# Two scratch tiles of their own, two loads traced later, and the last chunk of the output in halves, in a four-layer graph network kernel

## The chip, the cores and the metric

The kernel runs on one core of a Trainium2 chip. The time is that of the device in microseconds. Before the change it is 1733.46 us, the median of 3 runs (1733.0 to 1734.63).

## What is computed

Four layers on x [8, 2048, 64] with one adjacency `adj` [2048, 2048] of zeros and ones; after each layer `x = layernorm(x + layer(x))`. Cut to what matters here:

```python
# layer 0: hypergraph attention over H [2048, 64], and a mean over neighbours
industry = (adj / max(adj.sum(-1), 1)) @ (x @ W_ind)      # inverse degrees
g        = softmax-weighted sum over hyperedges of elu(beta * h + (1 - beta) * agg)
out      = softmax over the pair (industry, g), mixed
# layer 1: D^-1/2 (A + I) D^-1/2 x W^T
# layer 2: x, A x, (2 A A - I) x and softmax(relu(emb emb^T)) x, with weights made from emb per node
# layer 3: three steps of v = relu([v, adj @ v] W1^T + b1) W2^T + b2
```

## The kernel before, in words

**Tiling.** The eight batches are taken as four pairs p = 0..3, so that a pair's features fill 128 partitions. The 2048 nodes are 16 tiles of 128 (t) or 4 chunks of 512 (c). The product of an operand with `adj` runs over the 16 tiles, for two chunks at a time (g = 0, 1, both chunks in the two halves of one PSUM tile `ug` [128, 2, 512]), and twice over, for a rounded part `v{c}h` and its remainder `v{c}l` (`split`, L162).

**Order of the work.** The program traces instructions in the order in which the Python code makes them; a planner then orders each engine's queue, and lets an instruction that it takes to be ready pass others. `tc.keep_in_program_order` (in the code `pin`, and within `mm` and `transpose`) holds an instruction behind the one that was traced before it on the same engine. All matmuls are held that way. The loads by `load_emb` (L1066) and `load_xn` (L1027), and the instructions of `inverses` (L359), are not. `after(n, ...)` and `later(n, ...)` trace a piece n `tick`s later; a tick follows each matmul of a product.

**Stages, in order of time.** (1) Up to about 222 us, layer 0's attention: per tile and slot, TensorE adds three matmuls into `pz`, VectorE, ScalarE and GpSimd finish them (L815 to L825), and between them TensorE does the products of x with adj (`products`, L342) as filler. Within it `inverses` makes 1/sqrt(deg+1) (`dinv`, a power on GpSimd, L367) and 1/max(deg,1) (L368, L369), both through one tile `deg1`; later it turns the latter with TensorE and stores it (`inv_hbm`). (2) Up to about 470 us, the mixing of layer 0's two parts (`mix_*`, the loop at L1085, 16 steps), with the rest of the products and layer 1 (`layer1`, L1034) as filler. SyncE loads what a step needs: `uts`, `invs`, `gn`, `rs`. Ahead of the loop SyncE also loads the first chunk of the embeddings (`et`, L1073), which `make_er` and `make_el` round after the mixing. (3) Layer 1's tail; x after layer 1 goes to memory as `x2_hbm[p]` (L1018), and `load_xn` fetches it back into `xn[p]` over ScalarE's queue. (4) Layer 2: the softmax product, the products with adj (`supports`, L1262) with small pieces beside them (`aside`), among them `make_est` (L1352), which splits the embeddings for the per-node weights. Its tile `e_hi` takes its place in turn with all tiles of the tag `ut` (two buffers), which hold what leaves PSUM on its way to memory (`out_t`, L1231). Then the per-node weights and their products. (5) Layer 3, from about 1275 us: for each pair three steps of products, and in the last step `rectified` (L1840) and `finish` (L1726): a matmul of four blocks into `po`, the sum with x, a layernorm (L134) and two stores.

**The very end.** For the last pair's last two chunks (`very_end`, L1873) the two chunks run one after the other, 32 matmuls of 512 columns each:

```python
for mine in ([[c] for c in own] if very_end else [own]):
    for t in range(NT ...):
        for i in range(2):
            for c in mine:
                mm(u[c], lhsT=x_part[t // JT][i][:, t % JT, :], rhs=adj_c(t, c), ...)
    for k, c in enumerate(mine ...):
        rectified(c, u[c], bias, very_end)
        later(6 if very_end else 14 + 8 * k, lambda c=c, h=h[c], p=p: finish(p, c, h))
```

Of the kernel before, what the change touches and what calls it, by code (L numbers as in the profile page):

```python
# [56 lines left out]
def tile_gnn_fast(  # L57
# [41 lines left out]
    def cols(c, n=C):  # L99
        return slice(c * n, (c + 1) * n)  # L100
# [70 lines left out]
    def mm(*args, **kw):  # L171
        tc.keep_in_program_order(nc.tensor.matmul(*args, **kw))  # L172

    def transpose(dst, src):
        tc.keep_in_program_order(nc.tensor.transpose(dst, src, ident))  # L175
# [166 lines left out]
    def products():  # L342

        deg1 = hy.tile([P, NT], F32, name="deg1")

        def degrees(g):
            du = pph.tile([P, 2, C], F32, tag="ph", name=f"du{g}", bufs=2)
            for t in range(NT):
                for i in range(2):
                    mm(  # L350
                        du[:, i, :], lhsT=ones_r, rhs=adj_c(t, 2 * g + i), start=t == 0, stop=t == NT - 1
                    )
                    yield
            for i in range(2):
                c = 2 * g + i
                r = slice(c * P // NCH, (c + 1) * P // NCH)
                evacuate(deg4[r, :], du[r, i, :])

        def inverses():  # L359

            pdc = places["small"]([P, JT, P], "pdc")
            for j in range(JT):
                transpose(pdc[:, j, :], deg4[:, cols(j, P)])
            pdc = pdc.rearrange("p j (c r) -> p c j r", c=NCH)[:, :, :, 0]
            d1 = deg1.rearrange("p (c j) -> p c j", c=NCH)
            nc.vector.tensor_scalar(d1, pdc, 1.0, None, op0=ALU.add)
            nc.gpsimd.tensor_tensor(dinv, deg1, neg_half[:, :NT], ALU.pow)  # L367
            nc.vector.tensor_scalar(d1, pdc, 1.0, None, op0=ALU.max)  # L368
            nc.vector.reciprocal(deg1, deg1)  # L369
            for _ in range(20):  # L370
                yield
            for c in range(NCH):
                pt = places["small"]([P, C], "pinv")
                for j in range(JT):
                    k = c * JT + j
                    transpose(pt[:, cols(j, P)], deg1[:, k:k + 1].to_broadcast([P, P]))
                row = va.tile([P, C], F32, tag="ut", name="inv", bufs=2)
                nc.scalar.copy(row, pt)
                nc.sync.dma_start(inv_hbm[:, cols(c)], row)
                for _ in range(4):  # L380
                    yield

        for p in range(NP):
            for g in range(2):
                own = (2 * g, 2 * g + 1)
                ug = pph.tile([P, 2, C], F32, tag="ph", name="ug", bufs=2)
                u = {c: ug[:, c % 2, :] for c in own}
                turning = inverses() if p == 0 and g == 1 else iter(())
                for t in range(NT):
                    for i in range(2):  # L390
                        for c in own:
                            mm(
                                u[c], lhsT=part[t // JT][i][:, t % JT, :], rhs=adj_c(t, c),
                                start=t == 0 and i == 0, stop=t == NT - 1 and i == 1,
                            )
                            tick()
                            if t > 1:
                                next(turning, None)
                            yield
                    if p == NP - 1 and g == 1 and t % JT == JT - 1:  # L400
                        first_parts(t // JT, free)
                    if p + 1 < NP and t % JT == JT - 1:
                        c = t // JT
                        if g == 1:
                            parts(p + 1, c)
                        if g == 1 and c < 2 or g == 0 and c >= 2:
                            fetch(p + 1, (c + 2) % NCH)
                if p == NP - 1:

                    for t in range(g * NT // 2, (g + 1) * NT // 2):  # L410
                        onto_diagonal(t, nc.gpsimd, ALU.add)
                for c in own:
                    ut = va.tile([P, C], F32, tag="ut", name="ut", bufs=2)
                    nc.scalar.copy(ut, u[c])
                    nc.sync.dma_start(u0_hbm[p][:, cols(c)], ut)
                if p == 0 and g == 0:
                    yield from degrees(0)
                    yield from degrees(1)
# [434 lines left out]
    def wide(c):  # L853
        return slice(c * JT, (c + 1) * JT)
# [172 lines left out]
    def load_xn():  # L1027

        for p in range(NP - 1):
            if room and done[p] == NCH:  # L1030
                done[p] = 0
                nc.scalar.dma_start(xn[p], x2_hbm[p][:])

    def layer1(p):  # L1034

# [30 lines left out]
    def load_emb(c, et):  # L1066

        nc.sync.dma_start(et, emb_4[:, cols(c)])
        return et

    er_scope = ExitStack()
    erp = er_scope.enter_context(tc.tile_pool(name="er", bufs=1))
    ets = [load_emb(0, erp.tile([P, C], F32, tag="er", name="et", bufs=2))]  # L1073
    remaining = filler
    filler = all_pairs()
    mix_load(0)
# [7 lines left out]
    fill(4)  # L1084
    for i in range(steps + 1):  # L1085
        k = 9 if i > NCH else 8
        if i < steps:
            mix_scores(i)
            fill(k)
        if i > 0:  # L1090
            mix_end(i - 1)
            fill(k)
        if i + 1 < steps:
            mix_load(i + 2)
            mix_ind(i + 1)
            mix_g(i + 1)
            fill(k)
        if i < steps:
            mix_weigh(i)
            fill(k)  # L1100
# [250 lines left out]

    def make_est(c):  # L1352
        e = e_parts.pop(c)
        hi = va.tile([P, C], F32R, tag="ut", name="e_hi", bufs=2)
        pin(nc.scalar.copy(hi, e))
        signed_parts(e, e, hi, odd16)
        pin(nc.vector.tensor_scalar(hi, e, flip, None, op0=ALU.mult))
        pin(nc.sync.dma_start(est_hbm[:, cols(c)], hi.bitcast(F32)))
# [364 lines left out]
        xs = xn[p][:, wide(c), :]  # L1723
        nc.gpsimd.tensor_tensor(xs, xs, b2.to_broadcast([P, JT, P]), ALU.add)  # L1724

    def finish(p, c, h):  # L1726
        po = lps.tile([P, JT, P], F32, tag="mm", name="po", bufs=4)
        for j in range(JT):
            mm(po[:, j, :], lhsT=h[:, cols(j, P)], rhs=bd_o, start=True, stop=True)
        r = staged("r")  # L1730
        nc.vector.tensor_tensor(r, po, xn[p][:, wide(c), :], ALU.add)  # L1731
        layernorm(va, grouped(r), grouped(r), centred=True, small=l2, tag="ut", bufs=2)
        for b in range(2):
            (nc.scalar if b and p == NP - 1 and c == NCH - 1 else nc.sync).dma_start(
                out[2 * p + b, c * C:(c + 1) * C, :].rearrange("(t p) f -> p t f", p=P),
                r[:, :, b * F:(b + 1) * F],
            )

# [51 lines left out]
    def opening():  # L1790
# [46 lines left out]
                factor(int(n > 22), h[int(n > 22)], bd_e2, be)  # L1837
        return uo

    def rectified(c, src, bias, at_end):  # L1840
        h[c] = new_h(c)
        if c % 2 == 0 or at_end:
            nc.scalar.activation(h[c], src, AF.Relu, bias=bias)  # L1843
        else:
            nc.vector.tensor_scalar(h[c], src, bias, 0.0, op0=ALU.add, op1=ALU.max)

    waiting = list(waiting)
    for p in range(NP):
# [3 lines left out]
        for step in range(STEPS):  # L1852
# [4 lines left out]
            for g in range(2):  # L1857
                own = (2 * g, 2 * g + 1)
                if p == 0 and step == 0:
                    u = {c: opened[c] for c in own}  # L1860
                else:
                    ug = pph.tile([P, 2, C], F32, tag="ph", name="u", bufs=2)
                    u = {c: ug[:, c % 2, :] for c in own}
                    for c in own:
                        mm(u[c], lhsT=w_v, rhs=h[c], start=True, stop=False)
                        tick()
# [4 lines left out]
                        later(2 if g else 40, prepare)  # L1871

                very_end = last and g == 1 and p == NP - 1  # L1873
                for mine in ([[c] for c in own] if very_end else [own]):
                    for t in range(NT if p or step else 0):
                        if checks and t in (2, 7, 12):
                            check()
# [9 lines left out]
                    for k, c in enumerate(mine if p or step or g else []):  # L1887
                        rectified(c, u[c], bias, very_end)
                        if last:
                            at = 6 if very_end else 14 + 8 * k  # L1890
                            later(at, lambda c=c, h=h[c], p=p: finish(p, c, h))
                        else:

                            at = 8 + 6 * k if g == 1 else 18 + 16 * k
                            later(at, lambda c=c: factor(c, h[c], bd_e2, be))
                if g == 1 and last and p + 1 < NP:
                    factor(NCH - 1, h_next[NCH - 1], bd_e, None)
        h = h_next
# [749 lines left out]
```

## Time and profile before

| | before |
|---|---|
| median of 3 runs | 1733.46 us |
| the profiled execution | 1736.35 us, its span 1734.6 us |
| TensorE matmul busy | 1656.1 us, 95% of the span |
| VectorE, ScalarE, GpSimd busy | 48%, 34%, 33% |
| granted TensorE clock, mean | 0.987 |
| 0 to 60 us | TensorE busy 39.3 of 60 us |
| 60 to 240 us | TensorE 156.8, VectorE 141.8, GpSimd 135.9 of 180 us |
| 240 to 1700 us | TensorE 1440.1 of 1460 us |
| 1700 us to the end | TensorE 19.9 of 34.6 us |

A view of waits has, for each engine and line, who it waited for, with the microseconds in total, the number of times and the longest. A timeline row has start, duration, engine, line, operation, `out<-in` with the shapes, and in brackets the idle time of that engine before it and what ended it. A row of windows has the busy time of PE, PEld (weight loads), DVE (VectorE), ACT (ScalarE) and POOL (GpSimd) in a stretch, then the granted TensorE clock (1.00 is full), the share of DMA and GB/s. L172 is the helper of all matmuls, L175 that of all transposes, so that they are told apart by the names of their tiles.

### The profile page before, as it was taken

How to read it: one execution, taken by the hardware profiler on the slowest of the kernel's cores; microseconds unless marked ns; L12 is line 12 of the kernel's file. 1: busy time of each engine (PE TensorE's matmuls, PEld its weight loads, DVE VectorE, ACT ScalarE, POOL GpSimd, SP SyncE). 2: the span in 40 equal slices, each digit the busy share in tenths (PEclk: the TensorE clock that was granted, in tenths of full speed). 3: DMA queues.
4: the chain of work that ended last, by engine and by line, in shares of the span. 5: the costliest groups of instructions: out<-in, count | busy, mean ns of one | idle time of the engine just before them, and what ended most of it. 6: DMA issues, size and time to landing. Idle time of an engine off the chain costs nothing. (4 is left out here: it accounts for less than half of the span.)

```text
span 1734.6 us, 27974 instructions
## 1 busy us (share of the span) xinstructions
PE 1656.1 (95%) x11196; PEld 1206.1 (70%) x11196; DVE 833.3 (48%) x1532; ACT 589.4 (34%) x1031; POOL 570.6 (33%) x515
## 2 busy tenths in 40 slices
PE   6889899999989999999999999999989999999996
PEld 4667666666664444468788878888767877878775
DVE  7788945677742221210137147777533433433332
ACT  1346523434321212112213267878511222212221
POOL 4678835556534443422023001313210200202001
PEclk9899999999999999999999999999999999999998
DMA  9834334444340000027344467675571111211111
GB/s 351 277 121 127 124 116 138 154 140 145 106 129 6 31 27 4 24 70 291 118 134 131 114 149 158 137 165 129 149 263 48 50 55 43 61 49 43 55 43 39
DMA packets 171180, 195.83 MB, mean 113 GB/s; under 512 B 71536, under 2 KB 116336, under 8 KB 169760
## 3 DMA queue, kind: packets, MB, share of 16 engines
q1 hardware_dynamic: 160096, 154.54, 30.7%
q0 software_dynamic: 8544, 30.68, 5.3%
q10 hardware_dynamic: 2400, 8.72, 1.4%
q8 instruction: 90, 1.47, 0.4%
q14 instruction: 50, 0.41, 0.1%
HBM read 126.72 MB, written 67.17 MB: 112 GB/s over the span
## 5 line engine op out<-in xcount | busy, mean ns | idle before, releaser
L172 PE MATMUL ua<-pt,xn 128*128 128x512 f32 x512 | 230.2, 592 | 1.4 <-DVE pt L1174 1.4
L172 PEld LDWEIGHTS ua<-pt,xn 128*128 128x128 f32 x512 | 96.9, 190 | 111.1 <-issue 104.0
L1539 DVE COPY w_half<-pw 128x512 f32<-128x512 f32 x160 | 109.8, 705 | 87.5 <-PE pw L172 86.7
L1535 ACT COPY w_half<-pw 128x1024 f32<-128x1024 f32 x128 | 129.9, 1015 | 58.4 <-PE pw L172 58.3
L172 PE MATMUL py<-w_half,xg 128*32 128x128 f32 x4096 | 143.0, 280 | 1.7 <-issue 1.7
L172 PE MATMUL u<-adj,v0h 128*128 128x512 f32 x384 | 134.5, 428 | 1.1 <-ACT h L1843 1.1
L172 PE MATMUL u<-adj_more,v2h 128*128 128x512 f32 x384 | 125.3, 404 | 0.0
L172 PEld LDWEIGHTS py<-w_half,xg 128*32 128x32 f32 x4096 | 111.6, 138 | 19.5 <-issue 2.6
L172 PE MATMUL u<-adj,v0l 128*128 128x512 f32 x384 | 125.0, 403 | 0.0
L172 PE MATMUL u<-adj_more,v2l 128*128 128x512 f32 x384 | 123.4, 398 | 0.0
L1180 POOL TENSOR_TENSOR acc<-acc,pt 128x512 f32<-128x512 f32 x60 | 76.5, 1276 | 104.2 <-DVE pt L1174 103.5
L172 PE MATMUL pw<-est,wst 64*128 64x256 f32 x1024 | 110.4, 318 | 0.4 <-ACT w_half L1535 0.4
L1174 DVE TENSOR_SCALAR pt<-pt 128x512 f32<-128x512 f32 x64 | 29.9, 468 | 152.3 <-ACT pt L1173 152.1
L172 PEld LDWEIGHTS pw<-est,wst 64*128 64x128 f32 x1024 | 82.7, 186 | 25.4 <-ACT w_half L1535 18.9
L1752 ACT CAST ar<-fcav 128x512 fp32r<-128x512 f32 x64 | 39.5, 618 | 170.3 <-DMA fcav<-in_adj_t 169.3
L1753 DVE SCALAR_TENSOR_TENSOR ar<-fcav,ar 128x512 f32<-128x512 f32 x64 | 45.5, 710 | 103.4 <-ACT ar L1752 103.4
L1173 ACT ACTIVATE pt<-s 128x512 f32<-128x512 f32 x64 | 38.0, 598 | 164.5 <-PE s L172 164.5
L172 PE MATMUL u<-adj,v1h 128*128 128x512 f32 x288 | 93.7, 403 | 0.0
L172 PE MATMUL u<-adj_more,v3l 128*128 128x512 f32 x288 | 93.1, 398 | 0.2 <-DVE v3l L168 0.2
L172 PE MATMUL u<-adj_more,v3h 128*128 128x512 f32 x288 | 92.7, 400 | 0.0
L172 PE MATMUL u<-adj,v1l 128*128 128x512 f32 x288 | 92.0, 397 | 0.0
L1724 POOL TENSOR_TENSOR x<-x,rows 128x512 f32<-128x512 f32 x16 | 22.6, 1435 | 209.7 <-PE pt L175 127.7
(408 smaller groups left out, 3270.1 us busy)
## 6 DMA issues: line engine op xcount, KB each, us to landing
fcav<-in_adj_t SPq DMA_DIRECT2D x64, 256.0 KB, 3.0
u_hbm<-ut SPq DMA_DIRECT2D x48, 256.0 KB, 2.9
xg<-u_hbm SPq DMA_DIRECT2D x24, 512.0 KB, 7.0
adj<-in_adj_t POOLq DMA_DIRECT2D x16, 512.0 KB, 7.7
adj_more<-in_adj_t POOLq DMA_DIRECT2D x16, 512.0 KB, 7.0
adj_hbm<-adj_more SPq DMA_DIRECT2D x16, 512.0 KB, 6.5
x_hbm<-r SPq DMA_DIRECT2D x28, 256.0 KB, 2.4
hs_hbm<-st ACTq DMA_DIRECT2D x8, 584.0 KB, 6.7
```

Of the source, the lines that this page charges most:

```text
L172: tc.keep_in_program_order(nc.tensor.matmul(*args, **kw))
L1173: nc.scalar.activation(pt, s, AF.Exp)
L1174: nc.vector.tensor_scalar(pt, pt, 1.0, None, op0=ALU.max)
L1180: nc.gpsimd.tensor_tensor(accs[c], accs[c], pt, ALU.add)
L1535: pin(nc.scalar.copy(dst, pw.rearrange("p j o n -> p n (j o)")))
L1539: pin(copy(dst[:, :, 2 * j:2 * j + 2], bank.rearrange("p o n -> p n o")))
L1724: nc.gpsimd.tensor_tensor(xs, xs, b2.to_broadcast([P, JT, P]), ALU.add)
L1752: nc.scalar.copy(ar, seen_a)
L1753: nc.vector.scalar_tensor_tensor(ar.bitcast(F32), seen_a, 1.0, ar.bitcast(F32), op0=ALU.mult, op1=ALU.not_equal, accum_out=left[:, t, k:k ...
```

## The change

- `inverses` gets a second small tile `deg_inv` for 1/max(deg,1); before, it overwrote `deg1`, which the power on GpSimd reads.
- `load_xn` hands its load to `after(14, ...)`, so that it is traced 14 ticks later.
- The load of the first chunk of embeddings is traced within the mixing loop, at step 4, and not ahead of it.
- `e_hi` in `make_est` gets a tile of the pool `l2`, one per chunk (tag `g{c}`), and leaves the turn of `ut`.
- The very last chunk runs in two halves of 256 columns (`last_half`), from a PSUM tile `us` of its own, each half with its own 32 matmuls, its own rectification and its own `finish` over two blocks; `finish` takes a range of blocks. The chunk before it runs alone as before.

In the few words that come with it, the change also names a sooner return of the adjacency. `return_adj` (L1678) and its calls have no line in the diff.

```diff
     def products():
         deg1 = hy.tile([P, NT], F32, name="deg1")
+        deg_inv = hy.tile([P, NT], F32, name="deg_inv")
...
-            d1 = deg1.rearrange("p (c j) -> p c j", c=NCH)
+            d1, di = (d.rearrange("p (c j) -> p c j", c=NCH) for d in (deg1, deg_inv))
             nc.vector.tensor_scalar(d1, pdc, 1.0, None, op0=ALU.add)
             nc.gpsimd.tensor_tensor(dinv, deg1, neg_half[:, :NT], ALU.pow)
-            nc.vector.tensor_scalar(d1, pdc, 1.0, None, op0=ALU.max)
-            nc.vector.reciprocal(deg1, deg1)
+            nc.vector.tensor_scalar(di, pdc, 1.0, None, op0=ALU.max)
+            nc.vector.reciprocal(deg_inv, deg_inv)
...
-                    transpose(pt[:, cols(j, P)], deg1[:, k:k + 1].to_broadcast([P, P]))
+                    transpose(pt[:, cols(j, P)], deg_inv[:, k:k + 1].to_broadcast([P, P]))
...
             if room and done[p] == NCH:
                 done[p] = 0
-                nc.scalar.dma_start(xn[p], x2_hbm[p][:])
+                after(14, lambda p=p: nc.scalar.dma_start(xn[p], x2_hbm[p][:]))
...
-    ets = [load_emb(0, erp.tile([P, C], F32, tag="er", name="et", bufs=2))]
+    ets = []
...
     for i in range(steps + 1):
         k = 9 if i > NCH else 8
+        if i == NCH:
+            ets.append(load_emb(0, erp.tile([P, C], F32, tag="er", name="et", bufs=2)))
...
         e = e_parts.pop(c)
-        hi = va.tile([P, C], F32R, tag="ut", name="e_hi", bufs=2)
+        hi = l2.tile([P, 4, P], F32R, tag=f"g{c}", name="e_hi").rearrange("p a b -> p (a b)")
         pin(nc.scalar.copy(hi, e))
...
-    def finish(p, c, h):
-        po = lps.tile([P, JT, P], F32, tag="mm", name="po", bufs=4)
-        for j in range(JT):
-            mm(po[:, j, :], lhsT=h[:, cols(j, P)], rhs=bd_o, start=True, stop=True)
-        r = staged("r")
-        nc.vector.tensor_tensor(r, po, xn[p][:, wide(c), :], ALU.add)
-        layernorm(va, grouped(r), grouped(r), centred=True, small=l2, tag="ut", bufs=2)
+    def finish(p, c, h, blocks=(0, JT)):
+        first, end = blocks
+        n = end - first
+        po = lps.tile([P, JT, P], F32, tag="mm", name="po", bufs=4)[:, 0:n, :]
+        for j in range(n):
+            mm(po[:, j, :], lhsT=h[:, cols(first + j, P)], rhs=bd_o, start=True, stop=True)
+        r = staged("r")[:, 0:n, :]
+        nc.vector.tensor_tensor(r, po, xn[p][:, c * JT + first:c * JT + end, :], ALU.add)
+        layernorm(va, grouped(r), grouped(r), groups=2 * n, centred=True, small=l2, tag="ut", bufs=2)
         for b in range(2):
-            (nc.scalar if b and p == NP - 1 and c == NCH - 1 else nc.sync).dma_start(
+            (nc.scalar if b and first else nc.sync).dma_start(
...
+    def last_half(k, src):
+        part = slice(k * C // 2, (k + 1) * C // 2)
+        for t in range(NT):
+            for i in range(2):
+                mm(
+                    src, lhsT=x_part[t // JT][i][:, t % JT, :], rhs=adj_c(t, NCH - 1)[:, part],
+                    start=False, stop=t == NT - 1 and i == 1,
+                )
+                tick()
+        dst = h[NCH - 1]
+        nc.scalar.activation(dst[:, part], src, AF.Relu, bias=b1s)
+        later(6, lambda: finish(NP - 1, NCH - 1, dst, (k * JT // 2, (k + 1) * JT // 2)))
...
+                    if last and g == 1 and p == NP - 1:
+                        own = own[:1]
...
-                for mine in ([[c] for c in own] if very_end else [own]):
+                for mine in [own]:
...
+                if very_end:
+                    us = pph.tile([P, 2, C], F32, tag="ph", name="u", bufs=2)[:, :, 0:C // 2]
+                    for k in range(2):
+                        mm(us[:, k], lhsT=w_v, rhs=h[NCH - 1][:, cols(k, C // 2)], start=True, stop=False)
+                        tick()
+                    h[NCH - 1] = new_h(NCH - 1)
+                    for k in range(2):
+                        last_half(k, us[:, k])
```

## The prediction

> **What bounds the kernel now.** I read the page's first part, then all waits of TensorE, then the timeline and the windows round each wait that an edit touches, and last the chain at the end. TensorE is busy 95% of the span, so an edit pays only where TensorE stands. The waits that the edits bear on:
>
> ```profile
> PE pg L175 <- DMA gn<-gs_hbm: 4.0, 1, 4.0
> PE po L172 <- ACT ut L1057: 4.9, 2, 3.7
> PE pn L175 <- ACT ut L1235: 2.0, 1, 2.0
> PE u L172 <- ACT h L1843: 1.1, 1, 1.1
> ```
>
> Behind them stand these rows of the timeline (VectorE at 126, ScalarE at 490 and 836), and then the windows (the seventh number is the granted clock):
>
> ```profile
> 125.93 0.17 DVE L368 TENSOR_SCALAR deg<-pdc 128x16 f32<-128x16 f32 x1 [4.72 <-POOL dinv L367]
> 490.43 1.07 ACT L1057 COPY ut<-u 128x512 f32<-128x512 f32 x2 [7.92 <-issue]
> 835.75 0.59 ACT L1235 COPY ut<-u 128x512 f32<-128x512 f32 x1 [4.38 <-DMA est_hbm<-e_hi]
> ```
> ```profile
> 120.00:125.00 5.00, 3.39 (x16) 2.44 (x15) 1.21 (x2) 1.71 (x3) 4.92 (x4) 1.00 0.01 2
> 125.00:130.00 5.00, 2.81 (x10) 2.14 (x11) 4.07 (x11) 1.85 (x7) 4.05 (x4) 0.88 0.00 0
> 130.00:135.00 5.00, 5.00 (x21) 3.96 (x20) 4.38 (x9) 3.90 (x11) 3.89 (x4) 0.78 0.42 110
> ```
>
> And the chain that ended last, its final part:
>
> ```profile
> 1719.87 0.70 ACT h L1843
> 1720.57 0.04 issue
> 1720.62 1.17 PE po L172 x8
> 1721.79 0.02 issue
> 1721.81 0.70 DVE r L1731
> ...
> 1722.60 0.64 ACT ln_c L149
> 1723.23 0.02 issue
> 1723.26 0.70 DVE ln_v L151
> 1723.96 0.02 issue
> 1723.98 0.18 DVE ln_e L153
> ...
> 1724.79 1.15 POOL ln_r L155
> 1725.94 0.02 issue
> 1725.97 0.69 DVE r L156
> ```
>
> From the last product (ends 1719.84) to 1726.66, 6.82 us, there is no TensorE work but the small `po`; then come the stores and the end, 7.9 us, which nothing here changes much.
>
> **A: `deg_inv`.** One more tile, no instruction more. VectorE's L368 no longer waits for GpSimd's power (2.95 us, 122.95 to 125.90), which stood behind two sums `acc`. VectorE gets back up to 4.72 us; queued behind L368 were `y`, `pz` and the next slots, for which TensorE waited. TensorE's loss there: idle 1.59 and 0.99 us before rows at 126.21 and 127.47, and from the clock in the windows (0.12 + 0.22) x 5 = 1.7 us, together 4.3. But GpSimd is the next one late: it is busy 4.92 of 5 us in 120 to 125 with the same power, and its next `acc` (126.85) can come only 0.95 us sooner; three buffers of `y` let VectorE run ahead of it for a while. Bounds -4.7 and 0; I take the middle of 0.95 and 4.3, rounded up a little: **-2.8**.
>
> **B: `load_xn` 14 ticks later.** The third load waits on ScalarE's queue from 481.6 to 489.98 for the store of x2, and behind it stand the two copies `ut` at 490.43 for which TensorE waits 3.66 us (487.41 to 491.07). The clock then falls to 0.64 and 0.51 till 494: eight `po` and two `u` take 1.72 us, where the like row at 466 takes 0.92, and the next pair 1.00 for 0.56, 1.24 us together. At stake: 4.9. But the load is not held in traced order: the first of the three stands at 473.51, before the matmuls `pb` of 474.80, though it is traced after those of 480.48; and `fcav` for layer 3's checks (L1747) is issued at 458.12. A load goes where the planner finds it ready, and its place in the trace decides only between ready ones. The copies are already traced before it, and it passed them. So I take **0**, with -4.9 as the other end.
>
> **C: `et` inside mixing.** On SyncE, issues run without a gap from 230.07: `bp`, two `bd_w`, `et` at 231.75, `gn` at 232.44. Without `et` ahead, `gn` is issued 0.69 us sooner, and 256 KB less go before it. TensorE stands 4.03 us for it (233.6 to 237.63) and would stand 3.3. `et` then comes after the loads that are traced before it, in SyncE's gap at 235.8 or later; its cast `er` on ScalarE, for which ScalarE waited 5.95 us to 236.46 at no cost, moves with it. In mixing ScalarE has gaps of 2.5 us at each `t`, so at most some 3 us of such a wait come through. The Trainium skill (TensorE: Matmul & The Clock Gate, What's actually happening) has the clock halve after an idle window of about 3.4 us. Here it fell after 4.03 us (0.63, 0.50 and 0.90 in the three windows from 237.6 to 243.0: 0.5 + 1.0 + 0.2 = 1.7 us lost) and after 3.66 us, and stayed 1.00 after the 1.96 us at 836. By the rule a stop of 3.3 us might just escape: -2.4 in all; by the nearest row it doesn't. I take **-0.7**; ends -2.4 and +2.3 (3 us less 0.7).
>
> **D: `e_hi` out of the turn of `ut`.** The copy of 835.75 waited for the store of `e_hi` (issued at 831.34, taking 1.99 us on SyncE). In the new turn its buffer is that of the copy at 826.62, whose store was issued at 827.23, and a store lands in 2.4 us or so; it can go at about 831.4, right behind the one at 830.78. TensorE's 1.96 us go. Next late: the second copy (837.98), which needs the buffer stored at 833.90; it ends at 838.57, and TensorE, 1.96 us earlier than its 840.62, asks at 838.66. It just fits. **-2.0**, ends -2.0 and -1.
>
> **E: the last chunk in halves**, step by step against the rows:
> - Between the last two chunks, starts of matmuls are 1.52 us apart (1709.38, 1710.90) where 0.233 is usual: chunk 3 waits for ScalarE to read chunk 2 out of the same tile. The new `us` is another tile. But `finish` of chunk 2 now follows two own terms and four short matmuls, 1.0 us, and waits 0.3 for `h`. -1.29 + 0.3 = -1.0.
> - 32 matmuls of 512 columns at 0.233 (7.46 us) become 64 of 256. No row has this form. 512 columns take 0.233; 128 columns (`po`, eight in 0.89) 0.111. The skill's figure (same page, Back-to-back issue gap) is N/2.4 + 2.5 ns, 0.109 for 256 and 0.216 for 512, and would make it 7.0 us; but its rule for loads (LDWEIGHTS: 128 columns in 107 ns) speaks against halving, since each load has only half as long to hide. The rows lie above the first figure by 20 ns at 512 columns; 0.107 + 0.02 gives an estimate of 0.13. 64 x 0.13 = 8.3: +0.85; ends -0.5 (0.109) and +2.8 (0.16, the load's 0.053 of streaming unhidden). Own terms: +0.05.
> - The second half must wait for ScalarE to read the first, both being parts of one tile; that a tile's parts are not told apart is seen in `DVE h L1845 <- ACT h L1843` (43.4 us, 10 times: two readers of two chunks, one after the other). A drain of 0.29, 0.03, a relu of 0.38, 0.05, less 0.13: +0.62; 0 if they are told apart.
> - `po` of the first half, four instructions: +0.44.
> - The tail on half the width, from rows with 256 columns (ScalarE `bias<-pb` 0.37, VectorE L1153 0.42): relu -0.32, `po` -0.44, sum -0.28, square -0.26, reduction -0.28, scale -0.27. The power took 1.64 us on 8 columns and 2.95 on 16, so 0.98 on 4: -0.67. Together -2.5. The first half's chain ends 5 us after its product, before the second needs VectorE.
>
> Sum **-1.5**; ends -3.5 and +1.
>
> No line of `return_adj` is changed, so a sooner return is worth nothing. **The sum:** -2.8 + 0 - 0.7 - 2.0 - 1.5 = -7.0. On the profiled execution, 1736.35 (span 1734.6 and 1.75 round it), that is 1729.3; the median of the runs is 2.9 lower, and 1733.46 - 7.0 = **1726.5**.
>
> **The rivals.**
> 1. *The later load does pass behind the copies* (B counts). For it: ScalarE's queue is otherwise free there; against it, the moved loads above. -7.0 - 4.9: **1721.6**.
> 2. *GpSimd takes VectorE's place in A*, and the halves gain nothing. For it: POOL 4.92 of 5 us. -0.95 - 0.7 - 2.0 = -3.6: **1729.9**.
> 3. *The edits don't do what they say*: `et` again ahead of `gn` or its cast in front of a `t`, A and E as in 2. About -1.5: **1732**.
> 4. *Slower: the weight loads of the 64 short matmuls are not hidden at all.* Place: the last 10 us. LDWEIGHTS rows show 0.19 us; 0.19 + 0.107 = 0.30 each costs 64 x 0.17 = 10.9 more than my 0.13. It outweighs all else from 0.13 + 7.0/64 = 0.24 us each. Against it: `po` gets through a load and 128 columns in 0.111. **1737.4**.
>
> **How the numbers follow.** A measurement here tells about 0.2%, 3.5 us, from no change. The likeliest case, 42%: 1726.5, own range 1723.5 to 1729.5. Rival 1: 28%. Rival 2: 20%, half of it within 0.2%. Rival 3: 5%, within. Rival 4: 5%, slower. Faster: 0.42 x 0.95 + 0.28 + 0.10 = 0.78; same 0.17; slower 0.05. The range leaves out rival 4, the lowest third of rival 1 and a little of 2 and 3: 1718 to 1732.
>
> **What would show it.** A: L368 right behind L366, and POOL's idle time round 120 to 135 shrinking. B: whether copies L1057 stand before or behind the third load; a gap of 3.66 us left in TensorE says that nothing moved. C: `gn` issued next to `bd_w`, TensorE's wait near 3.3. D: no wait of `pn` near 836. E: starts of the short matmuls 0.13 us apart, no stop between chunks 2 and 3, one of some 0.6 between the halves, about 4.3 us from the last product to the last sum. I am wrong if new waits of TensorE on ScalarE or VectorE turn up in 240 to 480, from queues ordered anew.

## The result, and the profile after

The changed kernel takes 1727.86 us (median of 16 runs, 1724.46 to 1733.03) where the kernel before, on the same chip, took 1733.36 (16 runs). The ratio is 0.9968, with a 95% interval from 0.9959 to 0.9977: 5.5 us less, between 4.0 and 7.1. That is 1.4 us above the forecast of 1726.5 and inside its range. The profiled execution has a span of 1729.0 us (before 1734.6), and TensorE is busy 1655.4 us of it (1656.1 before): what went are stops of TensorE, not work. The total came out nearly as forecast, but two of its five terms did not, in opposite directions.

**Waits of TensorE after.** As before: what waits, for what, us in total, times, longest.

```profile
PE po L172 <- ACT ut L1058: 5.5, 3, 3.7
...
PE pinv L175 <- DVE y L820: 3.4, 2, 3.1
...
PE u L172 <- DVE v3l L168: 2.0, 1, 2.0
...
PE pg L175 <- POOL v0l L168: 1.1, 1, 1.1
...
PE u L172 <- ACT h L1856: 0.6, 1, 0.6
```

Of the four lines shown of before, `pg` fell from 4.0 us to 1.1 (C), `pn` is gone (D), and `u <- ACT h` is halved, as it now stands between two halves (E). The view puts the 1.1 us down to GpSimd, but `gn` landed at 234.60, 0.14 us before TensorE's start, and in c_et, where the view names `gn`, it was 0.13: `gn` would have held TensorE as long. `po` still waits 3.7 us (B); its third stop, 0.65 us at 357.91, is not there before. Two lines take a new place: `pinv` waits for VectorE (A), and `u` waits for `v3l` at the opening of layer 3.

**Timeline of VectorE and GpSimd after, round edit A.**

```profile
120.61 0.17 DVE L369 TENSOR_SCALAR deg_inv<-pdc 128x16 f32<-128x16 f32 x1
...
132.85 0.68 DVE L816 TENSOR_TENSOR pz<-pz,R 128x512 f32<-128x512 f32 x1
133.45 4.82 DVE L825 TENSOR_TENSOR y<-y,co 128x512 f32<-128x512 f32 x1
...
124.07 3.39 POOL L368 TENSOR_TENSOR dinv<-deg,neg_half 128x16 f32<-128x16 f32 x1
...
133.95 1.31 POOL L168 TENSOR_TENSOR hrl<-hrow,hrh 128x512 fp32r<-128x512 f32 x1
135.19 1.31 POOL L826 TENSOR_TENSOR acc<-acc,y 128x512 f32<-128x512 f32 x1
136.44 1.27 POOL L168 TENSOR_TENSOR v1l<-xc,v1h 128x512 fp32r<-128x512 f32 x1
```

L369 no longer waits: it runs at 120.61, where its like ran at 125.93. But 13 us later one product `y<-y,co`, whose two inputs lie in SBUF, is on record for 4.82 us. The 41 rows of its line have a median of 0.69. In that time GpSimd runs three operations without a gap (133.95 to 137.71), and the row ends 0.56 us behind the last of them. The longest row of the line in the kernel before, 3.45 us, ends 0.56 us behind two such operations too (169.98 and 169.42).

**Windows after, the stretch of edit A** (the last three numbers are granted clock, DMA share and GB/s):

```profile
120.00:125.00 5.00, 4.97 (x26) 3.86 (x25) 4.88 (x13) 2.34 (x6) 4.92 (x4) 1.00 0.01 2
125.00:130.00 5.00, 3.62 (x17) 2.48 (x16) 3.25 (x8) 3.04 (x10) 5.00 (x4) 1.00 0.00 0
130.00:135.00 5.00, 4.54 (x24) 3.51 (x24) 5.00 (x6) 3.10 (x6) 4.39 (x4) 1.00 0.55 168
135.00:140.00 5.00, 1.94 (x12) 1.41 (x11) 5.00 (x5) 1.03 (x2) 3.98 (x4) 0.97 0.41 116
140.00:145.00 5.00, 5.00 (x18) 3.77 (x17) 3.73 (x9) 3.62 (x12) 3.38 (x3) 0.69 0.83 284
```

In 120 to 130 TensorE is busy 8.59 us, before 6.20, and its clock stays at 1.00, before 0.88. In 135 to 140 it is busy only 1.94 us, before 4.91, and then the clock is 0.69. What the first windows win, the last ones give back.

**Timeline of ScalarE after, at edits B and D.**

```profile
486.17 0.33 ACTq L1033 DMA_DIRECT2D xn<-x_hbm  x1
486.61 1.07 ACT L1058 COPY ut<-u 128x512 f32<-128x512 f32 x2 [7.96 <-issue]
...
827.97 0.59 ACT L1238 COPY ut<-u 128x512 f32<-128x512 f32 x1
833.55 0.59 ACT L1238 COPY ut<-u 128x512 f32<-128x512 f32 x1 [4.99 <-DMA xt_hbm<-ut]
```

The third load still stands in front of the two copies (B did nothing). The copy that stood at 835.75 now runs at 827.97, without a wait. The one after it (837.98 before) is that of 833.55; it waits for another store, and TensorE has no wait for it.

**The end of the chain that ended last, after:**

```profile
1710.51 0.48 ACT h L1856
1710.99 0.04 issue
1711.04 0.98 PE u L172 x6
1712.01 0.45 PE po L172 x4
1712.46 3.12 PE u L172 x26
...
1715.60 0.48 ACT h L1856
...
1716.13 0.73 PE po L172 x4
...
1716.88 0.43 DVE r L1736
...
1719.10 0.53 POOL ln_r L155
...
1719.66 0.42 DVE r L156
```

From the last product (1715.58) to the last `r` (1720.08) it is 4.5 us, before 6.8. From there to the end of the span it is 8.9, before 7.9.

**A table by stage.** TensorE runs nearly the same matmuls in all these kernels. So each matmul of one trace can be paired with its like in the trace of before, and the difference of the two starts is the lead that the kernel has there. The table gives by how much the lead changes over each stage (negative is faster; stages by the time of before; each end is the median of the five starts before it; the last stage runs to the end of the span). The third column is the kernel that has that edit alone. The last gives the kernels with one edit that is not this stage's: it shows what one trace differs from another with no cause here.

| stage, us | changed kernel | that edit alone | others |
|---|---|---|---|
| A, 121 to 226 | -0.75 | -0.36 | -0.3 to +1.1 |
| C, 226 to 300 | -3.48 | -3.26 | -0.5 to +0.8 |
| B, 470 to 520 | +0.27 | +1.56 | -0.8 to -0.3 |
| D, 830 to 850 | -2.18 | -2.18 | -0.3 to +1.4 |
| opening of layer 3, 1273 to 1400 | +1.01 | | 0.0 to +1.7 |
| E, 1690 to the end | -1.19 | -1.36 | 0.0 to +0.2 |

The five edits make -7.3 us in the changed kernel. The rest of its -5.5 in the profile: +0.75 already there ahead of 121, the +1.0 of the opening, and next to nothing elsewhere. C, D and E stand clear of the last column. A lies barely under it, the opening lies inside it, and for B the column is too narrow a measure (b_load and c_slot, below).

### The profile page after: what moved, and what is told of

Read it like the earlier page. It is cut to its first block, busy times and chain, and to the rows that moved or that the text cites. A ratio compares the mean times of both kernels' runs of the same rounds, so it can differ in the third digit from the quotient of the medians.

```text
span 1729.0 us, 28043 instructions
## 1 busy us (share of the span) xinstructions
PE 1655.4 (96%) x11230; PEld 1208.0 (70%) x11230; DVE 843.0 (49%) x1536; ACT 589.1 (34%) x1033; POOL 569.9 (33%) x516
## 5 line engine op out<-in xcount | busy, mean ns | idle before, releaser
L172 PE MATMUL u<-adj,v0h 128*128 128x512 f32 (+1 forms) x388 | 135.7, 427 | 0.6 <-ACT h L1856 0.6
L172 PE MATMUL u<-adj,v0l 128*128 128x512 f32 (+1 forms) x388 | 125.8, 402 | 0.0
L172 PE MATMUL u<-adj_more,v2h 128*128 128x512 f32 (+1 forms) x388 | 125.7, 402 | 0.0
L172 PE MATMUL u<-adj_more,v2l 128*128 128x512 f32 (+1 forms) x388 | 124.0, 396 | 0.0
L172 PE MATMUL u<-adj_more,v3l 128*128 128x512 f32 (+1 forms) x291 | 93.5, 396 | 2.1 <-DVE v3l L168 2.0
L172 PE MATMUL u<-adj,v1h 128*128 128x512 f32 (+1 forms) x291 | 94.0, 401 | 0.0
L172 PE MATMUL u<-adj_more,v3h 128*128 128x512 f32 (+1 forms) x291 | 93.1, 398 | 0.0
L172 PE MATMUL u<-adj,v1l 128*128 128x512 f32 (+1 forms) x291 | 92.6, 395 | 0.0
```

## The experiments

All times come with runs of the kernel before on the same chip. The ratio turns them into us of 1733.4. "Theory" in the expectations is the reading of the result before the run:

| kernel | median us (before) | ratio, 95% interval | us |
|---|---|---|---|
| a_deg | 1734.44 (1735.2) | 0.9992 (0.9977 to 1.0006) | -1.4 |
| b_load | 1738.08 (1735.36) | 1.001 (0.9998 to 1.0022) | +1.7 |
| c_et | 1733.18 (1735.2) | 0.9982 (0.9971 to 0.9993) | -3.1 |
| d_ehi | 1733.27 (1735.2) | 0.9983 (0.9966 to 0.9999) | -2.9 |
| e_half | 1733.88 (1735.2) | 0.999 (0.9978 to 1.0002) | -1.7 |
| c_queue | 1731.37 (1735.36) | 0.9981 (0.997 to 0.9992) | -3.3 |
| c_slot | 1731.47 (1736.07) | 0.9979 (0.9969 to 0.9989) | -3.6 |
| f_power | 1727.55 (1735.36) | 0.9953 (0.9938 to 0.9968) | -8.1 |
| g_hold | 1728.32 (1735.36) | 0.9956 (0.9944 to 0.9968) | -7.6 |
| g2_last | 1727.49 (1736.07) | 0.9942 (0.992 to 0.9964) | -10.1 |
| h_consts | 1728.06 (1736.07) | 0.9957 (0.9943 to 0.9972) | -7.5 |
| i_all2 | 1721.92 (1736.07) | 0.9921 (0.9901 to 0.9941) | -13.7 |

An interval is 2 to 4 us wide on either side, which is as much as one edit is worth. So the times decide on the large ones, and the stages of the traces on the others. The five single edits add up to -7.4 us, with B the odd one out.

### Each edit alone: a_deg, b_load, c_et, d_ehi, e_half

Each is the kernel before with one part of the diff above and nothing else.

> Edit A alone, on the kernel before. Theory: TensorE gets ahead by up to 5 us at 132, and loses it again to two- or three-microsecond stops up to 141, because VectorE's sum of two tiles in SBUF is held while GpSimd works through its backlog; net 0 (-1 to +1 us) at the first `pi` near 226, and about 1733 in all. The prediction's term: -2.8, that is about 1730.5. Should the gain be lost in the whole change only because something else of it got in between, this run keeps -2.8 or more.

Its lead at 121, 132, 141 and 226 is -3.54, -8.69, -2.69 and -3.90: it wins 5.2 us, loses 6.0, and finds 1.2 again on the way to `pi`, the first products of mixing, near 226: -0.36 in all. The same course stands in the changed kernel (-5.1, +6.0) and in the three later kernels that keep the power where it is; these five end between -0.16 and -0.75. So nothing else in the change took A's gain. Its interval holds both 0 and -2.8 us; the traces decide here, and their -0.16 to -0.75 lies barely under what kernels without A show in this stage (-0.3 to +1.1).

> Edit B alone. Theory and prediction: 0 (-0.5 to +0.5 us); the third load of x2 stands again ahead of the two copies `ut` near 490, and TensorE again waits 3.7 us for them. The rival of the prediction, in which it passes behind them: -4.9.

The third load again goes out first, at 489.88 (before 489.98), and the copies follow at 490.32. TensorE waits 4.0 us for them. Both the theory and the prediction said 0; the ratio just includes it, and -4.9 is far outside. The 1.56 us that this stage loses come with a wait 0.3 us longer and a clock of 0.53 and 0.79 in 490 to 500 (before 0.66 and 1.00). c_slot, in which B is not made, differs from before by 3.0 us in this stage too, to the other side. So the stage varies by that much with no edit of its own, probably with the landing of its stores.

> Edit C alone. Theory: -3.3 to -3.6 us, 1730 in all, since `gn` lands in under 3 us after its issue once the 256 KB of `et` no longer stand ahead of it, and TensorE's stop of 4.03 us shrinks to about 1.1 with the clock kept at 1.00. The prediction's term: -0.7, only SyncE's issue slot, with a stop of about 3.3 us left.

TensorE's start after the stop for `gn` (its end is the wait in brackets, us <- releaser):

```profile
235.00 0.63 PE L175 MATMUL pg<-ident,gn 128*128 128x128 f32 x4 [1.39 <-DMA gn<-gs_hbm]
```

The stop was 4.03 us and is 1.39, and the clock stays at 1.00 from 225 to 245. The lead is -4.0 at 242. Some 0.8 is given back up to 260, where TensorE waits 0.51 us for the second `gn`. The time agrees (-3.1), and -0.7 is just outside its interval.

> Edit D alone: -2.0 us by the prediction and by the theory now, about 1731.3; TensorE's wait for the copies ahead of `pn` near 836 is gone. A rival has the copies wait for the next store instead, and gives -1 or less.

The wait of `pn` is gone from TensorE's list, and the stage gives -2.18, as in the changed kernel. The rival's -1 or less is inside the interval of the time, but not in this stage.

> Edit E alone: the prediction's term is -1.5, the traces of before and after show -1.4 from the last product of the third chunk to the last sum, and about +1 of it may be given back in the stores at the end, as more of them close together. So about -1.4 if the end of the program takes 7.9 us as before, -0.4 if it takes 8.9.

The stage gives -1.36, and in every kernel with this edit between -1.19 and -1.36. The end of the program, from the last `r` (1723.78) to the end of the span (1732.6), takes 8.8 us. So the products and the tail give 2.2 up to the last `r`, and 0.9 is given back behind it. The stores, which the expectation named, are not the reason: the last one of the changed kernel lands 3.1 us after its issue, before 3.3. The end hangs on another row, the last operation of GpSimd, first before and then after:

```profile
1724.30 1.64 POOL L155 TENSOR_TENSOR ln_r<-ln_e,neg_half 128x8 f32<-128x8 f32 x1 [4.96 <-DVE ln_e L153]
1718.62 1.01 POOL L155 TENSOR_TENSOR ln_r<-ln_e,neg_half 128x4 f32<-128x4 f32 x1 [2.41 <-DVE ln_e L153]
```

From the start of this row it is 10.3 us to the end of the span before and 10.4 after, and between 10.2 and 10.5 in all 14 traces, whether the row takes 1.64 us or 1.01. GpSimd's own queue fills this time: a branch, and a closing DRAIN that takes 6.20 us in each trace and ends 0.84 us ahead of the span. What is made shorter behind the start of that row, the power itself and the last `r`, does not bring the end nearer.

### What made `gn` late: c_queue and c_slot

```diff
-    ets = [load_emb(0, erp.tile([P, C], F32, tag="er", name="et", bufs=2))]
+    ets = [load_emb(0, erp.tile([P, C], F32, tag="er", name="et", bufs=2), nc.scalar)]
```

> The kernel before, with `et` loaded at its old place in the trace, but issued by ScalarE's queue and not by SyncE's. If the 256 KB of `et` ahead of `gn` are what made `gn` late, they still are, and TensorE's stop stays at 3.3 to 4 us: 0 to -0.7 us. If SyncE's issue slots made it late, the stop shrinks to 1 to 2 us as in the whole change: about -3.3.

The stop is 1.7 us and the stage gives -3.20. But this run tells nothing of the question: ScalarE issued `et` at 229.34, 2.5 us ahead of `gn` (231.84), so the bytes were out of the way as well. The expectation had taken the place of `et` in the queues to be unchanged. Hence c_slot, on top of edit C:

```diff
-    ets = []
+    et0 = erp.tile([P, C], F32, tag="er", name="et", bufs=2)
+    nc.sync.dma_start(et0[:, 0:16], emb_4[:, 0:16])
+    ets = []
```

> Edit C alone, with a second, small load at the old place of `et` on SyncE's queue: 16 columns of it, 8 KB in place of 256 KB, which the later load of the whole writes again. If the bytes ahead of `gn` made it late, TensorE stands 1.5 to 2 us for `gn` (1.4 in c_et, and an issue slot of 0.5 to 0.6 more), and about 2.7 of the 3.3 us are kept. If the issue itself did, the stop is 3.5 us or more again and nothing is kept.

```profile
235.23 0.63 PE L175 MATMUL pg<-ident,gn 128*128 128x128 f32 x4 [2.06 <-DMA gn<-gs_hbm]
```

The small load takes the same 0.58 us on SyncE as `et` did, and `gn` goes out at 232.03. TensorE starts 3.20 us after that. In the kernel before it started 5.19 us after the issue of `gn` (232.44 to 237.63). So with the issue in place and the bytes gone, 2.0 us of landing go, and the stage keeps -3.29. The issue alone is the 0.67 us between the stops of c_slot and c_et. So most of what the stop lost is the bytes. Why 256 KB cost 2.0 us stays open: at the 308 GB/s that the window of 235 to 240 shows they would take an estimated 0.85.

### Why A came to nothing: f_power

The changed kernel, with GpSimd's power in its own tile and ahead of mixing (the tile `deg1` goes):

```diff
-            d1, di = (d.rearrange("p (c j) -> p c j", c=NCH) for d in (deg1, deg_inv))
+            d1, di = (d.rearrange("p (c j) -> p c j", c=NCH) for d in (dinv, deg_inv))
             nc.vector.tensor_scalar(d1, pdc, 1.0, None, op0=ALU.add)
-            nc.gpsimd.tensor_tensor(dinv, deg1, neg_half[:, :NT], ALU.pow)
...
+    pin(nc.gpsimd.tensor_tensor(dinv, dinv, neg_half[:, :NT], ALU.pow))
```

> The changed kernel with GpSimd's power over the degrees taken out of the attention stage and put ahead of mixing, where its result is first read. If GpSimd's backlog of some 3 us is what gives A's gain back, TensorE keeps 2 to 4 us of it at the first `pi`: about 1725. If the sums of two SBUF tiles on VectorE collide with GpSimd's work whatever the power does, the gain stays lost: 1727.9.

The power now runs at 223.63 (2.97 us), where GpSimd has time. The lead at 121, 132, 141 and 226 is -0.01, -5.17, -2.38 and -4.01. Nearly the same 5 us are won, but only 2.8 of them are lost and not 6.0. That is 3.2 us less, about the power's 3.39, which may be chance: part of it is the clock. Windows of f_power, to be set beside those of the changed kernel:

```profile
130.00:135.00 5.00, 3.97 (x24) 3.05 (x22) 5.00 (x4) 1.11 (x3) 3.98 (x5) 1.00 0.43 119
135.00:140.00 5.00, 3.54 (x17) 2.78 (x18) 4.38 (x10) 3.24 (x10) 3.72 (x4) 1.00 0.78 247
140.00:145.00 5.00, 5.00 (x25) 4.09 (x24) 4.19 (x6) 3.11 (x7) 3.71 (x4) 1.00 0.72 235
```

TensorE has 3.54 us in 135 to 140 where it had 1.94, and the clock doesn't fall; in the changed kernel the fall costs an estimated (0.03 + 0.31) x 5 = 1.7 us, from its windows. The collision of VectorE and GpSimd is still there: one `y<-y,co` (130.38) is on record for 4.07 us, and 2.8 us are lost. So both readings have a part. That the power in this place costs 3.2 us at the first `pi` is shown. That the collision is what carries GpSimd's backlog over to VectorE is argued from the rows: a kernel without the collision was not made.

In time, f_power (0.9953) and the changed kernel (0.9968) have intervals that overlap. Of its lead of -6.3 at 300 it loses 1.3 by 360 and 3.7 at the opening of layer 3. The 4 us at the first `pi` are shown by two traces, this one and that of i_all2 (-4.12).

### The third load behind the copies: g_hold and g2_last

The changed kernel with the loads held behind what is traced before them on ScalarE:

```diff
-                after(14, lambda p=p: nc.scalar.dma_start(xn[p], x2_hbm[p][:]))
+                after(14, lambda p=p: pin(nc.scalar.dma_start(xn[p], x2_hbm[p][:])))
```

> The changed kernel with the deferred load of x2 held in its place in ScalarE's queue, so that it can't be issued ahead of the two copies `ut`. If the planner's order, and not the place in the trace, is why edit B did nothing, this takes away TensorE's 3.7 us before `po` and the lower clock after it: -4.9, about 1723. If another wait stands right behind that one, -1 to -2.

The lead goes from -3.20 at 486 to -8.47 at 496, which is the full price of B, and is back at -3.33 at 520. Timeline of g_hold (ScalarE's queue, VectorE, TensorE):

```profile
487.27 2.54 ACTq L1033 DMA_DIRECT2D xn<-x_hbm  x3
...
498.93 0.42 DVE L1156 TENSOR_TENSOR emb<-emb 128x256 f32<-128x256 f32 x1 [9.51 <-DMA emb<-in_emb]
...
505.69 4.63 PE L172 MATMUL ua<-pt,xn 128*128 128x512 f32 x5 [4.20 <-DVE pt L1177]
```

All three loads, 1 MB each, now go out at 487.27. The small load of `emb`, issued on SyncE at the same moment, lands behind them. VectorE stands 9.51 us for it, the norm of x and `pt` queue behind it, and TensorE waits 4.20 us for `pt` (1.4 before). So the planner's order is why B did nothing, and the next wait took nearly all of the gain. The other expectation had -1 to -2 left in that case; 0.1 of the 5.3 is left at 520. In g2_last only the third load is held:

```diff
-        for p in range(NP - 1):
+        for p in reversed(range(NP - 1)):
             if room and done[p] == NCH:
                 done[p] = 0
-                after(14, lambda p=p: nc.scalar.dma_start(xn[p], x2_hbm[p][:]))
+                after(14, lambda p=p: (pin if p == NP - 2 else (lambda d: d))(nc.scalar.dma_start(xn[p], x2_hbm[p][:])))
```

> The changed kernel with only the third of the three loads of x2 held behind the two copies `ut` (it is traced ahead of the other two for that). In g_hold all three were held and went out together, and the small load of `emb`, behind 3 MB, made VectorE wait 9.5 us. If that pile of loads is what gave the 5 us back, this kernel keeps 4 to 5 us at 520, and runs at about 1723. If any later third load is paid back at `pt`, it keeps 0 to 1 us: 1727.5.

The pile is gone and nothing is paid back at `pt`, but the stage gives only -1.4 us. The copies now wait for something else:

```profile
488.58 0.59 ACT L1058 COPY ut<-u 128x512 f32<-128x512 f32 x1 [6.10 <-DMA bias_hbm<-bias]
490.01 0.59 ACT L1058 COPY ut<-u 128x512 f32<-128x512 f32 x1 [0.85 <-DMA bias_hbm<-bias]
```

Their buffers come from the turn of `ut`, which `bias` has as well, and whose stores have to land first. TensorE's stop for them is 1.8 us, where it was 3.7, and the clock is 0.66 in 490 to 495. Neither expectation fits: the rest of the price stands under a second wait. One trace is little to go by here: in c_slot, where the load is not moved, this stop is 2.0 us, and the traced execution of g2_last (1730.82) is the second slowest of its six. The time, -10.1 us between -13.9 and -6.2, is better than the trace and too wide to tell.

### The opening of layer 3: h_consts

The call of `last_constants()` stands about 40 products later in the trace, after `own_term(3)`; nothing else is changed in the changed kernel.

> The changed kernel with the last constants of layer 3 traced some 40 products later, so that VectorE no longer waits 8.4 us for the load of `more` ahead of `v3l`. If that wait is the reason for the 1.8 us that the changed kernel loses at the opening of layer 3 (1274 to 1286), they stay: about 1726. If something else there is late, 1727.9.

Timeline of VectorE in h_consts:

```profile
1273.93 0.69 DVE L168 TENSOR_TENSOR v3l<-pr,v3h 128x512 fp32r<-128x512 f32 x1 [5.13 <-ACT v3h L167]
1274.60 0.17 DVE L114 MEMSET more<- 128x128 f32 x1
1277.63 0.29 DVE L128 TENSOR_REDUCE few<-more 128x1 f32<-128x128 f32 x1 [2.86 <-DMA more<-in_w_t]
```

`v3l` goes ahead of the wait for `more`, and TensorE has no wait for it. The stage gives -0.21 where the changed kernel loses 1.01. The other kernels with the old place lose between 0 and 3.7 here. From the issue of `more` to VectorE's start behind it there are 6.2 us in a_deg (which loses 0.1), 6.9 in g_hold (nothing), 8.0 in the changed kernel (1.0), 8.1 to 8.4 in e_half, c_et and b_load (0.8, 1.7 and 0.9) and 8.6 in f_power (3.7). So a load that lands late costs something, though not in strict order. In f_power the stop is 2.7 us, and the clock behind it 0.67 in 1280 to 1285, which makes an estimated 0.33 x 5 = 1.7 of its 3.7. Why the load lands later in some kernels is open. The time (-7.5) agrees, but doesn't tell this by itself from the changed kernel's -5.5.

### All three on top: i_all2

f_power, the third load as in g2_last and the constants as in h_consts, on the changed kernel.

> The changed kernel with three of the edits tried here: power out of the attention stage, third load of x2 held, last constants later. If their gains add up (about -2.6 to -4, -4 to -5, -1.8): 1717 to 1720. If each is absorbed by the next wait, no better than f_power: 1725 or more.

It is 0.9921 of the kernel before (0.9901 to 0.9941), some 13.7 us faster, and its interval lies wholly under that of the changed kernel. Scaled by the ratio to the first chip's 1733.4 it is 1719.7: the gains add up. By stages, A gives -4.12, C -2.90, B -4.23, D -2.18, the opening -1.04 and E -1.29. B is worth nearly its price here: the copies are on record at 478.41 and 479.86, and TensorE's stop for them is 0.3 us. They still wait for the `bias` stores, but from the issue of the first of these (472.56) to the first copy there are 5.9 us, in g2_last 7.4 (from 481.19); why is open. The traced execution is the fastest of its six (1718.08, the median 1721.92), so its stages promise more than the kernel gives in the median.

## Why the prediction was right, and where it was not

- **A, -2.8: wrong; -0.75 in the changed kernel, -0.5 in the mean of five.** The wait went as said, and 5 us were won, more than the upper bound of 4.7. The step that failed is "three buffers of `y` let VectorE run ahead of it for a while", and with it the middle between 0.95 and 4.3. GpSimd kept all its work (4.92 and 5.00 us in the two windows), and VectorE, now ahead, met it: in 130 to 140 VectorE is busy all the 10 us with 11 operations, before with 18 in 8.2. Rival 2 had named this, and its -0.95 for A is nearer. The price that neither had is the collision. The Trainium skill (SBUF — State Buffer, Summary: rules for kernel authors) says that of a VectorE operation with two inputs in SBUF and a GpSimd operation that reads SBUF, the second to issue blocks until the first has finished. The 4.82 us row fits it in part: it ends just behind GpSimd's last operation, but it starts 0.5 us ahead of the first of the three, while an indirect DMA of GpSimd is on record (132.95 to 133.93), and waits for all of them, not for one.
- **B, 0: right, and for the reason given.** The planner put the load where it was. That the planner, and not the place in the trace, sets the order is shown by g_hold and g2_last, where holding the loads moves them; what the planner takes to be ready is not shown. The -4.9 was a fair price for the wait (5.3 won in g_hold), but g_hold kept -0.1 of it at 520, and g2_last -1.4.
- **C, -0.7: the mechanism right, its size wrong; -3.5.** The step is "TensorE stands 4.03 us for it (233.6 to 237.63) and would stand 3.3". The text says that 256 KB less go before `gn`, and then counts only the 0.69 us of the issue. The stop became 1.12 us: of the 2.9 that went, 0.6 are the issue and 2.3 a shorter way from the issue of `gn` to TensorE (2.89 us, before 5.19), of which c_slot gives 2.0 to the bytes. With that the clock did not fall, and the 1.7 us that it was said to cost were not lost. A second stop for `gn`, 0.6 us at 241.75, gives a little back. The choice between rule and row at 3.3 us never came up here: a stop of 1.12 us is under both. At other stops it did (2.71 us in f_power, 2.81 in c_queue, 3.31 in c_et, the last two at `po`): the clock fell, as the row said.
- **D, -2.0: right; -2.18.** The first copy goes right behind the one before it (827.97 behind 827.49), and the second "just fits": TensorE has no wait left there.
- **E, -1.5: right in sum; -1.19.** The short matmuls start 0.12 us apart, estimated 0.13. The stop between chunks 2 and 3 is gone, and the one between the halves is there (0.56, estimated 0.62). From the last product to the last sum there are 4.5 us, estimated 4.3, and up to that point 2.2 are won. Up to the last product the halves cost 0.1 us, where the terms made 1.0; the 0.01 us that each short matmul takes less makes 0.6 of that. The step that failed is the end, which "nothing here changes much": from the last `r` it takes 1.0 us more. The end hangs on the start of GpSimd's last operation, 10.2 to 10.5 us ahead of it in every trace. So the terms for the power (-0.67) and the scaling (-0.27), both behind that start, shortened nothing that counts; together they are 0.94. Two errors of 0.9 us cancel here: that the sum came out is luck in part.
- **The sum, -7.0.** The edits' stages make -7.3, since C's error of -2.8 covers A's of +2.05. The forecast was near partly by that luck. The 1.4 us by which the time missed it lie where the prediction had no step: +0.75 ahead of the first edit, and the opening of layer 3, where TensorE meets a late load; neither is more than traces of other kernels differ by. The sign named for being wrong, new waits on ScalarE in 240 to 480, shows once, in the 0.65 us at 357.91; by 470 nothing of it is left (lead -3.5 at 300, -3.6 at 470).
- **The rivals.** Rival 4 is out: 0.12 us each, so the loads are hidden. Rival 1 is out by b_load and the trace. Rival 3 is out: `et` no longer stands ahead of `gn`. Rival 2 was right on A and wrong on the halves, which did gain.

## What to carry to other kernels

When a wait is removed from one engine, follow the engine that it waited for: if that one has no idle time, the gain lives as long as the buffers between them, and to keep it, its work has to move, as the power did here. When a load is taken from in front of another, count its bytes and the clock behind the stop, not only its issue. A load that is traced later need not be issued later unless it is held, and a load that is held may push others together. At the end of a program, find the engine that ends it: work that is saved on another one is not saved.

## What the runs showed of the hardware

- A VectorE operation with two SBUF inputs, 0.69 us in the median of its 41 rows, took 4.82 us beside back-to-back operations of GpSimd (4.07 in f_power). The longest row of the line in the kernel before, 3.45 us at another place, stands beside two such operations. These three rows end 0.56 to 0.57 us behind the last GpSimd operation beside them.
- 512-column matmuls start 0.233 us apart and 256-column ones 0.12, with a weight load of 0.19 us on record for each: halving the columns cost next to nothing here.
- The size of a load does not show in its issue: 8 KB took 0.58 us on SyncE, as 256 KB did. What differed was the time from the issue of the next load to its use, 3.2 and 5.2 us.
- After 60 us, the clock fell with every stop of TensorE of 2.7 us or more; the shortest are 2.71 (f_power, to 1278.66) and 2.81 (c_queue, to 486.28). It stayed at 1.00 after 1.12, 1.39, and 2.06 and 2.6 in c_slot. Shorter stops close together can do it as well: in the kernel before it fell behind 1.59 and 0.99 us (126 to 129). Until the end of the program, a fall is on record in each trace as half the clock for 3.41 us, or two or three times that, so each 3.41 us of it cost up to 1.7 us of matmuls.
- GpSimd's last operation starts 10.2 to 10.5 us ahead of the end in all 14 traces, and its closing DRAIN takes 6.20 of them.
